# One decoder layer with routed experts on one core: query and key weights merged on chip, fewer VectorE steps, results stored by SyncE

## The chip, the core and the metric

The kernel runs on one core of a Trainium2 chip. A core has five engines, each with an instruction queue of its own that is worked off in order: TensorE (PE; its weight loads are shown apart as PEld), VectorE (DVE), ScalarE (ACT), GpSimd (POOL) and SyncE (SP), which here only issues DMAs. Engines wait for each other through semaphores. Matmuls write to PSUM, everything else lives in SBUF, and the inputs, the results and two large tables of rows lie in HBM. The metric is the device time of one execution in microseconds (us).

## What is computed

A decoder layer over 16 sequences of 256 tokens with 256 features, all in float32. It has three parts, each followed by a residual and a layer norm:

```python
# 1. linear attention, 16 heads of 16: q, k = elu(.) + 1
x = norm(x + linear_attention(x, w_qkv, w_out, b_out))
# 2. cross-attention to 77 context rows a sequence, one head of 256
q = x @ Wq.T + bq
k = ctx @ Wk.T + bk
v = ctx @ Wv.T + bv
x = norm(x + softmax(q @ k.T) @ v)
# 3. a block with routed experts
a = attention(norm(x) * ln1_w + ln1_b)   # 16 heads of 16, 4 groups
h = x + a @ proj.T
y = norm(h) * ln2_w + ln2_b
gate = softmax(y @ router.T)             # 8 experts, the best 2
moe = sum over the best 2 of gate[e] * (gelu(y @ w1[e]) @ w2[e])
x = norm(x + h + moe)
```

In the attention of part 3 the causal axis is the sequence index (16), not the token: token t of sequence s sees token t of sequences 0 to s. So sequences are worked off in order, and the work of this attention grows with s.

## The kernel before

Four generators ("strands") are interleaved, each a step further on for one sequence: `beginning` (linear attention, `linear_attention`), `crossing` (`context_keys` for every second sequence, then `cross_attention`), `scoring` (`scores`: the projections of part 3 and the products of queries with all keys so far) and `routed` (`values`, then the router, then `place`). A scheduler fixes the order of each engine's queue when the program is built; scores and values carry a lower priority, the experts' blocks one lower still, so that they fill what the rest leaves.

**Cross-attention.** For each pair of sequences `context_keys` projects the context of both (154 columns) with the key weights on PE (tile pk) and adds the bias on DVE (L396, tile kT). Per sequence `cross_attention` projects the context's values, transposes x on PE, projects queries (pq from `wq_sb`), adds their bias on ACT (L411, tile q), multiplies q by kT (psc), takes the maximum on DVE (L417) and the exponential on ACT (L421), transposes it and multiplies by the values. All its PSUM tiles come from the pool `ps_x`, which has one buffer.

**Part 3's attention** runs on DVE: products and sums over 16 positions (L453, L497, L526). The sum of the exponentials divides the result at L528, on 512 elements a partition.

**Routing.** `router` finds the two best experts (L562, L563) and writes a mask `hot` (L565, L568). `place` gives each token a row in the table `slots_in`: it counts the tokens ahead with two bfloat16 matmuls (L600, L601), one over the current tile (m), one over all tiles before (cm, carried from sequence to sequence by L594 and L598), adds the expert's first row (L603), picks the two rows of each token (L607, L609), casts them (L611) and scatters (L616, indirect DMAs on POOL). `dispatch` and `pick` choose blocks of 128 rows for which an expert can run, and `experts` runs these: xs loaded by SP, transposed, two matmul layers (L287 as ph, L871 as po), rows stored to `slots_out` by SP. SP reads each block's place from a register first. `behind(...)` keeps SP's loads and stores in an order written out by hand.

**The end.** The sequences form two turns, of 13 and of 3 sequences. After a turn's experts, `combined` works on pairs of sequences: it gathers each token's two rows (L903, indirect DMAs on POOL, 52 and 12 of them), adds them to the residual on DVE (L916), and normalizes with `normalized(..., late=True)`: mean and variance on DVE, `shift` = -mean on DVE (L302), rstd on POOL (L303 adds epsilon, L308 takes the power -0.5, L311 multiplies the shift), the result on DVE (L316). `store` writes the pair to `out`, on POOL's queue (L924); only the last store goes by SP. POOL's and SP's queues are thus both shared between transfers and other work.

**Tables cleared.** The tables are cleared in pieces during `beginning`: `clear_piece` makes a tile of zeros from the layer norm's output on DVE (L251), so that each clearing DMA on SP starts only when that sequence is through.

Of the kernel before, what the change touches and what calls it, by code (L numbers as in the profile page):

```python
# [15 lines left out]
P = 128  # L16
# [22 lines left out]
W1S = 2  # L39
YS = 3  # L40
# [26 lines left out]
def decoder_kernel(  # L67
# [46 lines left out]
    def chunked(src, width, name):  # L114
        t = const.tile([P, src.shape[0] // P, width], FP, name=name)
        ins = load(t, src.rearrange("(c p) o -> p c o", p=P))
        return t, ins
# [22 lines left out]
    wk_sb, _ = chunked(wkT, D, "wk_sb")  # L140
    wv_sb, _ = chunked(wvT, D, "wv_sb")
    wq_sb, _ = chunked(wqT, D, "wq_sb")
# [67 lines left out]
    nc.gpsimd.tensor_copy(ones_c, ones)  # L210
    n_picks = max(k for turn in TURNS for of in picks(turn) for k in of)
# [3 lines left out]
    nc.vector.tensor_copy(count, count_i)  # L215

# [30 lines left out]
    def clear_piece(x1):  # L247
        if not to_clear:
            return
        zeros = one.tile([P, D], FP, tag="zeros", name=f"zeros_{len(to_clear)}")  # L250
        nc.vector.tensor_scalar(zeros, x1[:, 0, :], 0.0, None, ALU.mult)  # L251
        for rows_of in to_clear.pop(0):
            rows_of = rows_of.rearrange("(p r) d -> p r d", p=P)
            nc.sync.dma_start(
                out=rows_of, in_=zeros.unsqueeze(1).to_broadcast([P, rows_of.shape[1], D])
            )


    at_all = const.tile([P, S * NT, 2], FP_I, name="at_all")
    ws_all = const.tile([P, S * NT, NE], FP, name="ws_all")  # L260

# [27 lines left out]
    def normalized(dst, src, name, late=False, again=None):  # L289
# [12 lines left out]
        nc.vector.tensor_scalar(shift[:, :nt], mv[:, :nt, 0], -1.0, None, ALU.mult)  # L302
        nc.gpsimd.tensor_scalar(rstd[:, :nt], mv[:, :nt, 1], EPS, None, ALU.add)  # L303
# [7 lines left out]
        nc.gpsimd.tensor_tensor(shift[:, :nt], shift[:, :nt], rstd[:, :nt], ALU.mult)  # L311
        for i in range(n - 1, -1, -1):
            to = dst[i] if i < nt else again[i - nt]
            r, s = rstd[:, i : i + 1], shift[:, i : i + 1]
            if late:
                nc.vector.tensor_scalar(to, src[i % nt], r, s, ALU.mult, ALU.add)  # L316
            else:
                nc.scalar.activation(to, src[i % nt], AF.Identity, bias=s, scale=r)  # L318
# [14 lines left out]
    def linear_attention(b, xb):  # L333
# [52 lines left out]
        normalized(tiles(y), tiles(y), f"n1_{b}")  # L386
        return y

    def context_keys(b0, ct):

        pk = ps_x.tile([P, NC, 2 * CTX], FP, tag="pm", name=f"pk_{b0}")
        kT = two.tile([P, NC, 2 * CTX], FP, tag="kT", name=f"kT_{b0}")
        for j in range(NC):
            project(pk[:, j, :], lambda c: wk_sb[:, c, bass.ts(j, P)], lambda c: ct[:, c, :])
        for j in range(NC):
            nc.vector.tensor_scalar(kT[:, j, :], pk[:, j, :], bk[:, j : j + 1], None, ALU.add)  # L396
        return kT

    def cross_attention(b, x1, ct, kT):
# [6 lines left out]
        pq = ps_x.tile([P, NC, N], FP, tag="pm", name=f"pq2_{b}")  # L406
        for j in range(NC):
            project(pq[:, j, :], lambda c: wq_sb[:, c, bass.ts(j, P)], lambda c: xT[:, c, :])
        q = one.tile([P, NC, N], FP, tag="q2", name=f"q2_{b}")
        for j in range(NC):  # L410
            nc.scalar.activation(q[:, j, :], pq[:, j, :], AF.Identity, bias=bq[:, j : j + 1])  # L411
        yield
        psc = ps_x.tile([P, NT, CTX], FP, tag="pm", name=f"psc_{b}")
        for t in range(NT):
            project(psc[:, t, :], lambda c: q[:, c, bass.ts(t, P)], lambda c: kT[:, c, own])
        nmax = small.tile([P, NT], FP, tag="nmax", name=f"nmax_{b}")
        nc.vector.tensor_reduce(nmax, psc, AX.X, ALU.max, negate=True)  # L417
        p = one.tile([P, NT, CTX], FP, tag="p2", name=f"p2_{b}")
        total = small.tile([P, NT], FP, tag="total", name=f"total_{b}")
        for t in range(NT):  # L420
            nc.scalar.activation(  # L421
                p[:, t, :],
                psc[:, t, :],
# [77 lines left out]
    def values(s, x2, sc):  # L501
# [11 lines left out]
        nc.vector.reciprocal(total, total)  # L513
        yield
# [3 lines left out]
        with tc.high_priority(offset=-BULK):  # L518
# [8 lines left out]
        attn3 = attn.rearrange("p t (h d) -> p (t h) d", d=HD)  # L527
        nc.vector.tensor_tensor(  # L528
            attn3, attn3, total.unsqueeze(2).to_broadcast([P, NT * H, HD]), ALU.mult
        )  # L530
# [9 lines left out]
    def router(xT, top, hot, name):  # L540
# [23 lines left out]
        idx_f = small.tile([P, NT, 2], FP, tag="idx_f", name=f"idx_f_{name}")  # L564
        nc.vector.tensor_copy(idx_f, idx[:, :, :2])  # L565
        for t in range(NT):
            shape = [P, 2, NE]
            nc.vector.tensor_tensor(  # L568
                hot[:, t, :, :],
                count[:, :NE].unsqueeze(1).to_broadcast(shape),  # L570
                idx_f[:, t, :].unsqueeze(2).to_broadcast(shape),
                ALU.is_equal,
            )
# [12 lines left out]
    def place(u, d, b, t0, y4, hot, state):  # L586

        grid = [P, NT, NE]
        m = small.tile(grid, COUNT, tag="dm", name=f"dm_{b}")
        nc.vector.tensor_tensor(m, hot[:, :, 0, :], hot[:, :, 1, :], ALU.add)  # L590

        cm = two.tile([P, NT + 1, NE], COUNT, tag="dcm", name=f"dcm_{b}")
        if t0:
            nc.vector.tensor_copy(cm[:, 0, :], state["cm"])  # L594
        else:
            nc.vector.memset(cm[:, 0, :], 0.0)
        for t in range(NT):
            nc.vector.tensor_tensor(cm[:, t + 1, :], cm[:, t, :], m[:, t, :], ALU.add)  # L598
        pc = ps_b.tile([P, NT + 1, NE], FP, tag="pm", name=f"pc_{b}")
        nc.tensor.matmul(pc, lhsT=ones_c, rhs=cm, start=True, stop=False)  # L600
        nc.tensor.matmul(pc[:, :NT, :], lhsT=earlier_c, rhs=m, start=False, stop=True)  # L601
        slot = small.tile(grid, FP, tag="slot", name=f"slot_{b}")
        nc.vector.tensor_tensor(  # L603
            slot, pc[:, :NT, :], first_slot[u].unsqueeze(1).to_broadcast(grid), ALU.add
        )
        of = small.tile([P, NT, 2, NE], FP, tag="of", name=f"of_{b}")
# [426 lines left out]
```

## Time and profile before

| | |
|---|---|
| median of 3 runs | 821.78 us (819.98 to 822.94) |
| the profiled execution | 823.85 us, its span 822.0 us |
| busy: PE, PEld | 693.7 us, 552.2 us |
| busy: DVE, ACT, POOL | 601.9 us, 453.8 us, 303.1 us |
| mean granted clock of PE | 0.948 |
| HBM | 112.33 MB, 137 GB/s over the span |

The span runs from the first to the last instruction. A row of a group names the line, the engine and the operation, what it writes and reads, and how often; behind the bar stand the busy time and the mean of one (in ns), then the idle time just before. A float32 matmul stands as two records, a transpose as one. A line of a helper gathers all that the helper records (L287 is `project`), so groups are told apart by tiles. Durations of short instructions on one engine overlap: what a small step costs there is nearer to the distance of two starts.

### The profile page before, as it was taken

What the parts mean: (1) busy time and instruction counts of PE and PEld (TensorE: products, weight loads), DVE (VectorE), ACT (ScalarE), POOL (GpSimd) and SP (SyncE); (2) the same over time, 40 slices, a digit from 0 to 9 for tenths busy, and PEclk for the clock granted to TensorE, in tenths of its full rate; (3) what the DMA queues carried; (4) which work ended last, traced back from release to release, by engine and by line L of the source; (5) the groups of instructions that cost most, each with busy time, mean ns of one, the idle gap of its engine ahead of it and who ended that gap; (6) DMA issues with size and microseconds to landing.
All of it is one profiled execution on the core that took longest, in us unless ns stands there. A gap on an engine that the chain in (4) does not pass through costs nothing. (4 is left out here: it accounts for less than half of the span.)

```text
span 822.0 us, 12778 instructions
## 1 busy us (share of the span) xinstructions
PE 693.7 (84%) x3676; PEld 552.2 (67%) x3676; DVE 601.9 (73%) x1571; ACT 453.8 (55%) x967; POOL 303.1 (37%) x400
## 2 busy tenths in 40 slices
PE   6888878798899798989998989989789998989700
PEld 4656656566676676867786877768677887789600
DVE  2345758868898998979899978989899940334444
ACT  2354535545656667564956566485865665545300
POOL 2023224334343423334323332231333211588765
PEclk9999989989999999999999989999999999999955
DMA  8946454364353251721353412413333221555533
GB/s 279 392 166 217 139 188 151 102 204 156 104 198 115 85 193 41 241 72 66 119 164 110 134 52 90 129 58 122 91 103 88 95 70 66 167 178 152 161 107 101
DMA packets 98115, 112.33 MB, mean 137 GB/s; under 512 B 6336, under 2 KB 90560, under 8 KB 98048
## 3 DMA queue, kind: packets, MB, share of 16 engines
q1 hardware_dynamic: 90704, 90.81, 33.6%
q0 software_dynamic: 7344, 20.72, 7.9%
q8 instruction: 31, 0.51, 0.3%
q14 instruction: 36, 0.29, 0.1%
HBM read 39.42 MB, written 72.09 MB: 136 GB/s over the span
## 5 line engine op out<-in xcount | busy, mean ns | idle before, releaser
L287 PE MATMUL ph<-xsT,w 128*128 128x128 f32 (+1 forms) x976 | 160.9, 309 | 6.8 <-ACT xsT L831 3.5
L871 PE MATMUL po<-we_sb,h 128*128 x624 | 158.7, 386 | 6.2 <-ACT ys L879 2.3
L287 PEld LDWEIGHTS ph<-xsT,w 128*128 128x128 f32 x976 | 135.3, 193 | 21.9 <-ACT xsT L831 9.4
L616 POOL DMA_INDIRECT slots_in<-y,at_all x64 | 77.4, 1210 | 167.2 <-ACT h L862 35.8
L871 PEld LDWEIGHTS po<-we_sb,h 128*128 128x128 f32 x624 | 111.5, 193 | 22.5 <-issue 2.7
L453 DVE TENSOR_TENSOR qk<-q,k_all 128x128 f32<-128x128 f32 (+15 forms) x64 | 82.3, 1285 | 18.9 <-ACT k_all L481 18.2
L862 ACT ACTIVATE h<-ph 128x512 f32<-128x512 f32 x78 | 46.5, 597 | 85.1 <-PE ph L287 78.8
L453 DVE TENSOR_TENSOR pv<-sc,v_all 128x128 f32<-128x128 f32 (+15 forms) x64 | 82.9, 1295 | 0.4
L497 DVE TENSOR_REDUCE sc<-qk 128x8 f32<-128x128 f32 (+15 forms) x64 | 81.8, 1278 | 0.8
L526 DVE TENSOR_REDUCE attn<-pv 128x128 f32<-128x128 f32 (+15 forms) x64 | 81.6, 1275 | 0.5
L743 POOL TENSOR_TENSOR x<-x,y 128x512 f32<-128x512 f32 x16 | 27.6, 1728 | 134.9 <-DVE y L537 134.9
L815 ACT COPY w<-we_sb 128x1024 f32 x61 | 63.9, 1047 | 10.7 <-PE ph L287 9.6
L287 PE MATMUL pkv<-wqkv_sb,tT_x 128*128 128x512 f32 x128 | 61.4, 602 | 0.0
L287 PE MATMUL pq<-wqkv_sb,tT_n 128*128 128x384 f32 x128 | 54.1, 547 | 8.2 <-ACT tT_n L467 4.6
L384 POOL TENSOR_TENSOR x<-xb,rows_sb 128x512 f32<-128x512 f32 x16 | 24.5, 1533 | 81.1 <-DVE x L441 47.7
L308 POOL TENSOR_TENSOR rstd_n<-rstd_n,neg_half 128x2 f32<-128x2 f32 (+1 forms) x57 | 51.2, 898 | 4.4
L831 ACT ACTIVATE xsT<-px,cols_sb 128x256 f32<-128x256 f32 (+1 forms) x80 | 41.0, 564 | 13.0 <-PE px L828 13.0
L903 POOL DMA_INDIRECT r<-slots_out,at_all x36 | 35.4, 983 | 32.2 <-issue 32.2
L303 POOL TENSOR_SCALAR rstd_n<-mv_n 128x2 f32<-128x2 f32 (+1 forms) x57 | 19.6, 344 | 72.4 <-DVE mv_n L299 68.7
L318 ACT ACTIVATE x<-x,shift_n,rstd_n 128x256 f32<-128x256 f32 x64 | 35.0, 593 | 10.4 <-POOL shift_n L311 10.2
L316 DVE TENSOR_SCALAR res<-res,rstd_n,shift_n 128x256 f32<-128x256 f32 x32 | 11.7, 424 | 38.5 <-POOL shift_n L311 38.5
L287 PEld LDWEIGHTS pq<-wqkv_sb,tT_n 128*128 128x128 f32 x128 | 24.9, 209 | 22.0 <-ACT tT_n L467 6.3
(257 smaller groups left out, 1389.8 us busy)
## 6 DMA issues: line engine op xcount, KB each, us to landing
slots_out<-zeros SPq DMA_DIRECT2D x10, 3328.0 KB, 12.0
we_sb<-in_w SPq DMA_DIRECT2D x16, 512.0 KB, 9.0
slots_in<-zeros SPq DMA_DIRECT2D x2, 3328.0 KB, 12.3
xs<-slots_in SPq DMA_DIRECT2D x44, 128.0 KB, 2.1
slots_out<-ys SPq DMA_DIRECT2D x44, 128.0 KB, 1.8
xs<-slots_in SPq DMA_DIRECT2D x17, 256.0 KB, 2.8
slots_out<-ys SPq DMA_DIRECT2D x17, 256.0 KB, 2.2
xb<-in_x SPq DMA_DIRECT2D x16, 256.0 KB, 2.8
```

The source lines that it names most:

```text
L287: nc.tensor.matmul(dst, lhsT=lhsT(c), rhs=rhs(c), start=(c == 0), stop=(c == NC - 1))
L308: nc.gpsimd.tensor_tensor(rstd[:, :n], rstd[:, :n], neg_half[:, :n], ALU.pow)
L318: nc.scalar.activation(to, src[i % nt], AF.Identity, bias=s, scale=r)
L453: nc.vector.tensor_tensor(pr, a.to_broadcast(shape), b.to_broadcast(shape), ALU.mult)
L497: nc.vector.tensor_reduce(scr[:, :, r, :], pr, AX.X, ALU.add)
L526: nc.vector.tensor_reduce(attnr[:, :, r, :], pr, AX.X, ALU.add)
L616: scatter = nc.gpsimd.indirect_dma_start(out=scatters[u][2 * (t0 + t) + i], out_offset=bass.IndirectOffsetOnAxis(ap=at[:, t, i : i + 1], a ...
L815: nc.scalar.copy(w.rearrange("p c f -> p (c f)"), we_sb[:, bass.ds(off, NC * FF)])
L831: nc.scalar.activation(xT[:, c, : nt * P], px[:, c, : nt * P], AF.Identity, bias=ln2_b[:, c : c + 1], scale=ln2_w[:, c : c + 1],)
L862: nc.scalar.activation(h[:, fs.start : fs.stop, at], ph, AF.Gelu_apprx_tanh)
L871: nc.tensor.matmul(po[:, t, :], lhsT=h[:, f, bass.ts(t, P)], rhs=we_sb[:, bass.ds(off + (NC * FF + f * D), D)], start=(f == 0), stop=(f == ...
L903: nc.gpsimd.indirect_dma_start(out=r[:, t, i, :], out_offset=None, in_=slots_out[u], in_offset=bass.IndirectOffsetOnAxis(ap=at_all[:, b * ...
```

## The change

The kernel is changed in these places.

- **One matrix for queries and keys.** q k^T = (x Wq^T + bq)(c Wk^T + bk)^T = x (Wq^T Wk) c^T + x Wq^T bk + (bq Wk) c^T + bq bk. `merged_weights` makes Wq^T Wk and the bias parts on chip, once, before the first keys: eight transposes, fourteen small matmuls, copies on DVE. kT then has a third row of tiles, the part that depends only on the context row, repeated over all partitions. The query projection and its bias go; x transposed is multiplied by kT itself, and DVE adds the third row before the maximum (p). kT's bias is added on ACT. `wk_sb` and `wq_sb` are loaded into buffers that other tiles use later.
- **Fewer DVE steps.** `hot` in one compare without a cast; the counts ahead are carried in the row number itself (`state["next"]`, a row more in `slot`), so that cm goes and a third count matmul comes; the rows are summed straight into integers; the softmax of part 3 is divided before the values instead of after; zeros are made once; late norms use (x - mean) * rstd, with epsilon added on DVE and only the power left to POOL.
- **Results by SP.** `store` goes to SP's queue. In turn 0 it holds eight sequences back (LATE pairs) and puts the rest behind the loads; the remaining ones follow the last expert store.

```diff
+LATE = 4
...
-    wk_sb, _ = chunked(wkT, D, "wk_sb")
+    wk_sb, _ = chunked(wkT, D, "wk_sb", one, "q2")
+    wq_sb, _ = chunked(wqT, D, "wq_sb", one, "attnb")
     wv_sb, _ = chunked(wvT, D, "wv_sb")
-    wq_sb, _ = chunked(wqT, D, "wq_sb")
...
+    zeros = const.tile([P, D], FP, name="zeros")
+    nc.gpsimd.memset(zeros, 0.0)
+
+    def clear_piece(after):
...
-        zeros = one.tile([P, D], FP, tag="zeros", name=f"zeros_{len(to_clear)}")
-        nc.vector.tensor_scalar(zeros, x1[:, 0, :], 0.0, None, ALU.mult)
...
+            tc.add_manual_dep(ins.ins, after.ins.name, landed, reason="bandwidth")
...
-        nc.vector.tensor_scalar(shift[:, :nt], mv[:, :nt, 0], -1.0, None, ALU.mult)
-        nc.gpsimd.tensor_scalar(rstd[:, :nt], mv[:, :nt, 1], EPS, None, ALU.add)
+        if late:
+            nc.vector.tensor_scalar(rstd[:, :nt], mv[:, :nt, 1], EPS, None, ALU.add)
+        else:
+            nc.vector.tensor_scalar(shift[:, :nt], mv[:, :nt, 0], -1.0, None, ALU.mult)
+            nc.gpsimd.tensor_scalar(rstd[:, :nt], mv[:, :nt, 1], EPS, None, ALU.add)
...
-        nc.gpsimd.tensor_tensor(shift[:, :nt], shift[:, :nt], rstd[:, :nt], ALU.mult)
+        if not late:
+            nc.gpsimd.tensor_tensor(shift[:, :nt], shift[:, :nt], rstd[:, :nt], ALU.mult)
...
-                nc.vector.tensor_scalar(to, src[i % nt], r, s, ALU.mult, ALU.add)
+                nc.vector.tensor_scalar(to, src[i], mv[:, i, 0:1], r, ALU.subtract, ALU.mult)
...
+    def merged_weights():
+        wT = []
+        for w, name in ((wk_sb, "wk"), (wq_sb, "wq")):
+            t = two.tile([P, NC, D], FP, tag="sc", name=f"{name}T")
+            nc.vector.tensor_copy(t, transposed(ps_a, w, name))
+            wT.append(t)
+        wkT_, wqT_ = wT
+        for c in range(NC):
+            pm = ps_a.tile([P, D + 1], FP, tag="pm", name=f"pm_{c}")
+            own = bass.ts(c, P)
+            project(pm[:, :D], lambda d: wkT_[:, d, own], lambda d: wqT_[:, d, :])
+            project(pm[:, D:], lambda d: wkT_[:, d, own], lambda d: bq[:, d : d + 1])
+            nc.vector.tensor_copy(m_sb[:, c, :], pm[:, :D])
+            nc.vector.tensor_copy(mq_sb[:, c, :], pm[:, D:].to_broadcast([P, P]))
+        pb = ps_a.tile([P, NC + 1], FP, tag="pm", name="pm_b")
+        for c in range(NC):
+            own = bass.ts(c, P)
+            project(pb[:, c : c + 1], lambda d: wqT_[:, d, own], lambda d: bk[:, d : d + 1])
+        project(
+            pb[:, NC:],
+            lambda d: bq[:, d : d + 1].to_broadcast([P, P]),
+            lambda d: bk[:, d : d + 1],
+        )
+        nc.vector.tensor_copy(mb_sb, pb)
...
-            project(pk[:, j, :], lambda c: wk_sb[:, c, bass.ts(j, P)], lambda c: ct[:, c, :])
-        for j in range(NC):
-            nc.vector.tensor_scalar(kT[:, j, :], pk[:, j, :], bk[:, j : j + 1], None, ALU.add)
+            project(pk[:, j, :], lambda c: m_sb[:, c, bass.ts(j, P)], lambda c: ct[:, c, :])
+        project(pk[:, NC, :], lambda c: mq_sb[:, c, :], lambda c: ct[:, c, :])
+        for j in range(NC + 1):
+            nc.scalar.activation(kT[:, j, :], pk[:, j, :], AF.Identity, bias=mb_sb[:, j : j + 1])
...
-        pq = ps_x.tile([P, NC, N], FP, tag="pm", name=f"pq2_{b}")
-        for j in range(NC):
-            project(pq[:, j, :], lambda c: wq_sb[:, c, bass.ts(j, P)], lambda c: xT[:, c, :])
-        q = one.tile([P, NC, N], FP, tag="q2", name=f"q2_{b}")
-        for j in range(NC):
-            nc.scalar.activation(q[:, j, :], pq[:, j, :], AF.Identity, bias=bq[:, j : j + 1])
...
-            project(psc[:, t, :], lambda c: q[:, c, bass.ts(t, P)], lambda c: kT[:, c, own])
+            project(psc[:, t, :], lambda c: xT[:, c, bass.ts(t, P)], lambda c: kT[:, c, own])
+        nc.vector.tensor_tensor(p, psc, kT[:, NC, own].unsqueeze(1).to_broadcast(shape), ALU.add)
...
+        nc.vector.tensor_tensor(
+            sc3, sc3, total.unsqueeze(2).to_broadcast([P, NT * H, n]), ALU.mult
+        )
...
-        nc.vector.tensor_tensor(
-            attn3, attn3, total.unsqueeze(2).to_broadcast([P, NT * H, HD]), ALU.mult
-        )
...
-        cm = two.tile([P, NT + 1, NE], COUNT, tag="dcm", name=f"dcm_{b}")
...
-        nc.tensor.matmul(pc, lhsT=ones_c, rhs=cm, start=True, stop=False)
+        nc.tensor.matmul(pc, lhsT=ones_c, rhs=behind_none, start=True, stop=False)
+        nc.tensor.matmul(pc[:, NT, :], lhsT=ones_c, rhs=m[:, 0, :], start=False, stop=False)
         nc.tensor.matmul(pc[:, :NT, :], lhsT=earlier_c, rhs=m, start=False, stop=True)
...
+        first = state["next"] if t0 else first_slot[u]
+        nc.vector.tensor_tensor(slot, pc, first.unsqueeze(1).to_broadcast(shape), ALU.add)
+        state["next"] = slot[:, NT, :]
...
-        nc.vector.tensor_copy(at, at_f)
-        total = small.tile([P, NE], FP, tag="cnt_f", name=f"cnt_f_{b}")
-        nc.vector.tensor_copy(total, pc[:, NT, :])
...
-        def store(pair, queue=nc.gpsimd):
-            for b in pair:
-                queue.dma_start(out=out[b].rearrange("(t p) d -> p t d", p=P), in_=acc[b])
+            owed.extend((b, acc[b]) for b in pair)
+
+        def store(most, after):
+            while len(owed) > most:
+                b, of = owed.pop(0)
+                with behind(after[-1:]):
+                    nc.sync.dma_start(out=out[b].rearrange("(t p) d -> p t d", p=P), in_=of)
...
-                if i == 0 and n > 1:
-                    store(pairs[n - 2])
             if n:
                 add(pairs[n - 1])
+            if b1 < S:
+                store(2 * LATE, loads)
+            elif n == 0:
+                store(0, stores)
             yield
-        if len(pairs) > 1:
-            store(pairs[-2])
         add(pairs[-1])
-        store(pairs[-1], nc.sync if b1 == S else nc.gpsimd)
+        if b1 == S:
+            store(0, stores)
```

## The prediction

> **What bounds the kernel now.** I read the busy rows of the page first: which engine is full, and when.
>
> ```profile
> PE   6888878798899798989998989989789998989700
> ...
> DVE  2345758868898998979899978989899940334444
> ...
> PEclk9999989989999999999999989999999999999955
> ```
>
> Each digit is a fortieth of the span (20.5 us). PE and DVE are both near nine tenths from slice 10 to 31, counted from 0; neither alone is the bound. After slice 37 PE does nothing, while the span goes on for 46 us. Busy time by stage gives the sizes (columns: time, PE, PEld, DVE, ACT, POOL, granted clock, DMA):
>
> ```profile
> 200.00:640.00 440.00, 404.96 (x2097) 321.99 (x2097) 400.84 (x911) 284.46 (x601) 146.59 (x172) 0.98 0.36 115
> ...
> 704.00:776.00 72.00, 69.34 (x459) 62.44 (x457) 31.52 (x100) 36.90 (x58) 58.15 (x67) 0.98 0.54 162
> 776.00:823.00 47.00, 0.00 (x0) 0.00 (x0) 21.72 (x70) 0.85 (x2) 29.15 (x40) 0.54 0.36 115
> ```
>
> In the middle stage PE is 92% busy and DVE 91%: work taken from one alone would leave the other in the way. Work taken from both should come through. From 704 us on the chain of waits names POOL almost throughout: 64 gathers of expert rows, in order on one queue. The POOL timeline of the end shows what stands between them (start, length):
>
> ```profile
> 781.48 1.03 POOL L903 DMA_INDIRECT r<-slots_out,at_all  x1 [0.18 <-issue]
> 782.53 1.06 POOL L308 TENSOR_TENSOR rstd_n<-rstd_n,neg_half 128x4 f32<-128x4 f32 x1
> ...
> 793.97 0.72 POOL L308 TENSOR_TENSOR rstd_n<-rstd_n,neg_half 128x2 f32<-128x2 f32 x1
> 794.77 0.19 POOL L311 TENSOR_TENSOR shift_n<-shift_n,rstd_n 128x2 f32<-128x2 f32 x1
> 796.03 0.77 POOL L924 DMA_DIRECT2D out<-res  x1 [1.07 <-DVE res L316]
> 797.11 1.07 POOL L903 DMA_INDIRECT r<-slots_out,at_all  x1 [0.31 <-issue]
> ```
>
> The 52 gathers of turn 0 begin at 703.73 and end at 782.5; the 12 of turn 1 wait until 797.11 behind three normalizations and five stores of results. The last of the 61 expert stores (L885) starts at 783.3; with its 0.36 us and the 1.9 us to landing that these stores take in the middle, rows are there at 785.6, so 11.5 us of the end are queue order alone.
>
> **The change part by part.** The groups by shape give durations (busy us, mean ns):
>
> ```profile
> L287 PE MATMUL pq<-tT_x,wq_sb 128*128 128x256 f32 x128 | 34.4, 409 | 0.1
> ...
> L528 DVE TENSOR_TENSOR attn<-attn,total 128x512 f32<-128x512 f32 x16 | 11.0, 688 | 0.2
> ...
> L396 DVE TENSOR_SCALAR kT<-pk,cols_sb 128x154 f32<-128x154 f32 x16 | 5.6, 356 | 0.0
> ...
> L598 DVE TENSOR_TENSOR dcm<-dcm,dm 128x8 bf16<-128x8 bf16 x32 | 5.1, 159 | 0.6
> ```
>
> *PE in the body.* The query projection goes: 8 records a sequence. In the PE timeline such a run starts at 31.72 and the next work at 33.55, so 1.83 us, times 16 is 29.3. Added per pair of sequences is a third context projection, half of the 1.21 us that the 8 records of pk take at 70.19, times 8 is 4.8. Added per sequence is a count matmul of 8 columns: its nearest rows, pc at 640.01 and 640.04, start 0.03 apart but show 0.18 plus a weight load of 0.10, so between 0.03 and 0.28; I take 0.1, as they run back to back, times 16 is 1.6. Net: 29.3 - 4.8 - 1.6 = 22.9 us less PE.
>
> *DVE in the body.* Small steps cost their spacing, not their duration: `slot` 229.56 minus 0.10, `of` 229.67, about 0.10 apart while each row says 0.16 to 0.19. Per sequence go two dcm adds, one dcm copy, the casts idx_f and at_f, the copy cnt_f, and one of two hot compares: 7 x 0.10 x 16 = 11.2 (17 by durations). kT moves to ACT: 5.6. The zeros (L251) go: 4.3. The division by the softmax sum works on 32n elements instead of 512: the nearest row, the subtraction on the same tile, has a median of 0.46 against 0.688, so 16 x 0.23 = 3.7. Added is p = psc + bias over 154 elements, between L417 (0.311) and L396 (0.356) on the same shape: 16 x 0.33 = 5.3. The rstd step that the late normalization moves to DVE replaces the shift step there. Net: 11.2 + 5.6 + 4.3 + 3.7 - 5.3 = 19.5 us less DVE.
>
> *ACT.* L411 goes (13.6 us); 24 kT evictions come, at 0.39 each (between 128x77 with 0.325 and 128x256 with 0.476): 9.3. ACT is 65% busy in the middle, so I cost the move at nothing; PE and DVE hide it. If that cover were gone, a kT that is 3 x 0.39 instead of 2 x 0.33 late costs 0.5 us a pair, 4 us in all.
>
> *What comes through.* The lesser saving is 19.5; with each engine full for about 0.9 of the body, and the static queues between them, I take 16. Bounds: 0, if the freed time all becomes waiting, and 26, if the shorter chain (no query projection, no 0.84 us bias step on ACT at 33.76 between transposes and scores) also takes waits away.
>
> *The start.* The PE queue of the changed kernel puts the merging of the weights between po of sequence 0 and the transposes of sequence 1, and nothing else can pass: sequence 0 waits for kT, sequence 1 stands behind it.
>
> ```profile
> 22.14 3.59 PE L287 MATMUL po<-wout_sb,tT_a 128*128 128x256 f32 x8 [0.68 <-ACT tT_a L282]
> 25.53 0.73 PE L276 MATMUL pt_x<-ident,xb 128*128 128x128 f32 x4
> 26.99 1.99 PE L287 MATMUL pq<-tT_x,wqkv_sb 128*128 128x256 f32 x8 [0.73 <-DVE st_n L298]
> ```
>
> Eight transposes: 2 x 0.73 = 1.5. Four matmuls of 256 columns, 8 records: 2.0. Ten of one column, 20 records, by the nearest row (pl, 8 columns, 8 records in 1.06): 2.65. The first kT, now here: 1.2 + 0.6. Exposed on DVE: one 128x512 copy 0.69, one 128x256 eviction 0.42, and four hand-overs of some 0.2: 1.9. Together 9.9. The old kT's wait for its weights (1.78) and its 0.69 no longer stand before the keys of sequence 0: 9.9 - 2.5 = 7.4; I take 8. Bounds: 3, since PE had 4.7 us idle from 30 to 60 that can absorb part, and 14, since the first row above shows 3.59 for the work that takes 1.99 elsewhere, so PE's part of 8 can cost nearly twice as much.
>
> *The end.* POOL loses 15 stores (0.78 each), the rstd and the shift steps, and keeps pow. 52 gathers at their spacing of 1.25 are 65.0, with four pows of 1.1 between them 69.4 instead of 78.8. From there the old chain takes 14.6 to 797.11; without shift, store and its wait of 1.07, the gather follows the last pow (794.7 instead of 797.1), and two earlier rounds lose 0.2: 12. So the last gathers could start 81.4 us after the first instead of 93.4. The last expert store lands 81.9 after it, and becomes the later one: 11.5 saved, less 0.5 that the new SP work may cost it. I take 11.
>
> *SP's queue.* It takes 15 more stores. Two pairs stand before the store of ys_1_0 and before the second of ys_1_1; behind them wait these, the loads xs_1_7 and xs_1_8, and through three ys buffers ACT and PE. Pair 0 is normalized about 18 x 1.25 + 2.5 = 25 us after the first gather, pair 1 about 40 after. In the PE timeline px of block pairs 7 and 8 run 51 and 58 after it, ys_1_4 is wanted at about 51: cover of 10 us and more, so I cost it at nothing; gone, each us goes to the last store. The other stores stand behind all expert stores. Bounds for the end: 12 saved, or 0.
>
> Sum against the profiled execution's own 823.85 (span 822.0 and 1.85 around it): 823.85 - 16 + 8 - 11 = 804.85. The median of the runs is 2.07 lower, 821.78; in its terms 802.8, forecast as 803.
>
> **A rule that speaks against it.** PE's granted clock falls after idle stretches (columns as before):
>
> ```profile
> 285.00:290.00 5.00, 2.47 (x9) 1.17 (x8) 4.60 (x22) 4.41 (x13) 1.13 (x3) 0.86 0.10 35
> 290.00:295.00 5.00, 5.00 (x19) 3.57 (x18) 4.52 (x11) 3.90 (x10) 1.53 (x2) 0.80 1.04 348
> ```
>
> PE was idle 2.5 us, and 0.14 x 5 + 0.20 x 5 = 1.7 us of clock went. About ten such places are in the trace. The Trainium skill, "TensorE: Matmul & The Clock Gate", "Why this matters for your kernels", says to leave no gaps of over about 3 us between bursts, since one idle window puts the clock back to half. By that rule, if every sequence's hole passed the length, the sum would be 802.8 + 27 = 830; by the row, 802.8, until a gap opens.
>
> **Rivals.**
> - *Only the end counts.* The body is bound by waits between strands, its freed work turns idle (4 of 16 come). For it: PE's idle time has a dozen causes, the largest pt_n waiting for ACT with 10.1 us in the middle. Against: the two full rows. 823.85 - 4 + 8 - 11 = 816.9, or 814.8 against the median.
> - *Slower: clock.* Nothing of the body comes through, and the hole of the query projection becomes a dip in each of 16 sequences: 16 x 1.7 = 27. 823.85 + 27 + 8 - 11 = 847.9, or 845.8. It decides from 11 more dips on, where the forecast's 19 is eaten. Against: experts' matmuls fill PE from 250 us on.
> - *The end doesn't do what it says.* The normalizations come later than the cover, SP holds back expert stores, and the end saves nothing: 815.9, or 813.8.
>
> **How the numbers follow.** Forecast 0.66, only the end 0.13, end unchanged 0.10, slower 0.11. A difference within 0.3% (2.5 us) can't be told here. The forecast's own range is its bounds less their extremes, 788 to 813. To leave out no more than two in ten, the range goes from 786 (body 26, start 3, end 12 gives 786.8) to 821. Of the milder cases 0.05 may end within 0.3%: faster 0.84, same 0.05, slower 0.11.
>
> **What would show it.** PE's busy time falls by some 17 (22.9 less the 1.5 + 2.0 + 2.65 of merging), DVE's by some 17 to 20 (19.5 less the merging's copies). The transposes of sequence 1 start near 33.5. The first gather of turn 0 comes near 696 instead of 703.73, the first of turn 1 some 82 after it. SP's stores wait for DVE without PE starving between px 6 and 8. Wrong would be: more low clocks in the middle, or PE idle grown by as much as its work fell.

## The result, and the profile after

The changed kernel takes 816.24 us (median of 20 runs, 811.84 to 824.34), the kernel before 824.32 us beside it (20 runs, 818.99 to 829.07). The ratio is 0.9912, 95% interval 0.9891 to 0.9932: 0.9% less, or some 7 us (the medians lie 8 us apart). One of the changed kernel's runs, 824.34 us, was a slow one and is left out of the ratio. Forecast were 19 us. The profiled execution took 818.29 us with a span of 816.4, against 823.85 and 822.0 before: 5.6 us less.

The page of the changed kernel, busy times (time, share, records):

```profile
PE 691.5 (85%) x3632; PEld 546.3 (67%) x3632; DVE 589.3 (72%) x1451; ACT 449.7 (55%) x961; POOL 287.0 (35%) x369
...
PE   6888898788889899989998989989788998796940
...
DVE  1245875877896888989898988989978972153555
...
PEclk9899997998996999989999999999989999998985
```

PE's busy time fell from 693.7 to 691.5 us, not by the 17 that the prediction counts. The records did go (3676 to 3632). The ones that are left run longer: the row PEclk has seven digits under 9 up to slice 36 where the row before has three. The same stages as before, in windows (time, PE, PEld, DVE, ACT, POOL, granted clock, DMA):

```profile
200.00:640.00 440.00, 397.95 (x2053) 314.54 (x2052) 384.98 (x801) 275.94 (x587) 142.98 (x169) 0.96 0.34 109
704.00:776.00 72.00, 63.11 (x421) 56.77 (x420) 32.34 (x104) 36.58 (x56) 53.48 (x55) 0.95 0.53 155
...
776.00:823.00 47.00, 8.58 (x47) 7.11 (x45) 20.49 (x65) 2.75 (x5) 17.36 (x19) 0.68 0.39 125
```

In the middle PE lost 7 us of busy time and DVE 16, at a clock of 0.96 instead of 0.98. And PE now works past 776 us, where it was done before.

Four marks split the span; the body is taken from the transposes of sequence 1 to the first gather, the end from there to the last instruction:

| mark (us) | before | after | difference |
|---|---|---|---|
| transposes of sequence 1 | 25.53 | 34.16 | +8.6 (forecast +8) |
| body | 678.2 | 669.6 | -8.6 (forecast -16) |
| first gather of turn 0 | 703.73 | 703.73 | 0 |
| end | 118.3 | 112.7 | -5.6 (forecast -11) |

The busy times of the body, first before, then after (columns as above):

```profile
25.53:703.73 678.20, 607.66 (x3158) 478.19 (x3157) 543.68 (x1384) 410.01 (x897) 209.65 (x270) 0.97 0.39 129
34.16:703.73 669.57, 594.54 (x3073) 464.14 (x3071) 528.01 (x1255) 403.25 (x887) 208.49 (x268) 0.95 0.39 126
```

The start is as foreseen, the body and the end give half. The PE timeline of the start, changed kernel (start, length):

```profile
25.36 1.06 PE L288 MATMUL pt_wk<-ident,wk_sb 128*128 128x128 f32 x4
...
28.52 1.13 PE L299 MATMUL pm<-wqT,wkT 128*128 128x256 f32 x4 [1.07 <-DVE wqT L413]
...
34.16 0.60 PE L288 MATMUL pt_x<-ident,xb 128*128 128x128 f32 x4
```

Four transposes cost 1.06 us where the last line shows 0.60 for four: the clock is at half here. The POOL timeline of the end, changed kernel:

```profile
776.60 0.96 POOL L940 DMA_INDIRECT r<-slots_out,at_all  x1 [0.31 <-issue]
777.58 1.04 POOL L323 TENSOR_TENSOR rstd_n<-rstd_n,neg_half 128x4 f32<-128x4 f32 x1
784.61 1.11 POOL L323 TENSOR_TENSOR rstd_n<-rstd_n,neg_half 128x4 f32<-128x4 f32 x1 [5.98 <-DVE rstd_n L315]
788.75 0.69 POOL L323 TENSOR_TENSOR rstd_n<-rstd_n,neg_half 128x2 f32<-128x2 f32 x1 [3.04 <-DVE rstd_n L315]
791.52 1.01 POOL L940 DMA_INDIRECT r<-slots_out,at_all  x1 [2.08 <-DMA out<-res]
```

The stores are gone from POOL's queue, and in their place POOL waits for DVE: 5.98 and 3.04 us. So its last three powers are as far apart as before (7.0 and 4.1 us against 6.9 and 4.5). The first gather of turn 1 comes 87.8 us after the first of turn 0 (forecast 82, before 93.4).

### The profile page after: what moved, and what is told of

The parts are those of the page before. It is cut to its first block, busy times and chain, and to the rows that moved or that the text cites. A ratio compares the mean times of both kernels' runs of the same rounds, so it can differ in the third digit from the quotient of the medians.

```text
span 816.4 us, 12518 instructions
## 1 busy us (share of the span) xinstructions
PE 691.5 (85%) x3632; PEld 546.3 (67%) x3632; DVE 589.3 (72%) x1451; ACT 449.7 (55%) x961; POOL 287.0 (35%) x369
## 5 line engine op out<-in xcount | busy, mean ns | idle before, releaser
L299 PE MATMUL ph<-xsT,w 128*128 128x128 f32 (+1 forms) x976 | 163.9, 315 | 14.1 <-ACT ys L916 6.2
L908 PE MATMUL po<-we_sb,h 128*128 x624 | 156.3, 387 | 7.1 <-ACT xsT L868 3.0
L299 PEld LDWEIGHTS ph<-xsT,w 128*128 128x128 f32 x976 | 138.4, 199 | 29.7 <-ACT xsT L868 8.9
L498 DVE TENSOR_TENSOR pv<-sc,v_all 128x128 f32<-128x128 f32 (+15 forms) x64 | 84.6, 1322 | 0.6
L299 PE MATMUL pq<-wqkv_sb,tT_n 128*128 128x384 f32 x128 | 58.2, 584 | 9.4 <-ACT tT_n L512 8.3
L323 POOL TENSOR_TENSOR rstd_n<-rstd_n,neg_half 128x2 f32<-128x2 f32 (+1 forms) x57 | 50.2, 881 | 17.2 <-DVE rstd_n L315 13.1
L940 POOL DMA_INDIRECT r<-slots_out,at_all x36 | 35.2, 976 | 33.0 <-issue 27.2
L294 ACT COPY tT_a<-pt_a 128x512 f32<-128x512 f32 x32 | 18.7, 584 | 46.8 <-PE pt_a L288 46.7
L288 PE MATMUL pt_n<-ident,y 128*128 128x128 f32 x128 | 21.2, 289 | 27.3 <-ACT y L334 27.3
L299 PEld LDWEIGHTS pq<-wqkv_sb,tT_n 128*128 128x128 f32 x128 | 26.7, 223 | 24.6 <-ACT tT_n L512 10.3
```

What stands on the lines that cost most here:

```text
L299: nc.tensor.matmul(dst, lhsT=lhsT(c), rhs=rhs(c), start=(c == 0), stop=(c == NC - 1))
L323: nc.gpsimd.tensor_tensor(rstd[:, :n], rstd[:, :n], neg_half[:, :n], ALU.pow)
L498: nc.vector.tensor_tensor(pr, a.to_broadcast(shape), b.to_broadcast(shape), ALU.mult)
L908: nc.tensor.matmul(po[:, t, :], lhsT=h[:, f, bass.ts(t, P)], rhs=we_sb[:, bass.ds(off + (NC * FF + f * D), D)], start=(f == 0), stop=(f == ...
L940: nc.gpsimd.indirect_dma_start(out=r[:, t, i, :], out_offset=None, in_=slots_out[u], in_offset=bass.IndirectOffsetOnAxis(ap=at_all[:, b * ...
```

## The experiments

Ratios are to the kernel before, with 95% intervals. Clock is the median over the runs of the mean granted clock. Body and end (first gather of turn 0 to first of turn 1) come from one profile each, in us.

| kernel | ratio | clock | body | end |
|---|---|---|---|---|
| before | 1 | 0.949, 0.947 | 678.2 | 93.4 |
| the change | 0.9912 (0.9891 to 0.9932) | 0.941 | 669.6 | 87.8 |
| merged matrix alone | 1.0096 (1.0068 to 1.0125) | 0.934 | 679.3 | 93.9 |
| change without it | 0.9876 (0.9845 to 0.9907) | 0.960 | 682.3 | 86.0 |
| the end alone | 0.9932 (0.9903 to 0.9961) | 0.951 | 678.5 | 86.5 |
| query projection back, unread | 1.0360 (1.0330 to 1.0391) | 0.933 | 707.7 | 87.0 |
| LATE = 7 | 0.9901 (0.9866 to 0.9936) | 0.940 | 665.7 | 86.4 |
| merging in PE's gaps | 0.9831 (0.9791 to 0.9870) | 0.948 | 668.2 | 87.2 |
| matmuls in the gaps | 1.0044 (1.0020 to 1.0068) | 0.953 | 675.4 | 88.4 |
| no merging, LATE = 7, order | 0.9902 (0.9864 to 0.9939) | 0.957 | 675.6 | 86.3 |

**The parts, one by one.** Merged matrix alone, on the kernel before:

> The kernel before with the merged weight matrix alone; the DVE steps, the late norm, the zeros and the stores stay as before. By the prediction's terms: PE 24.5 us less in the body (29.3 - 4.8), DVE about the same (kT 5.6 goes, p 5.3 comes), start +8. Theory A (PE and DVE are both full, only what both lose comes through): the body gains about nothing, so 5 to 9 us slower than before. Theory B (PE's work counts by itself): 10 to 16 us faster than before. Theory C (PE's freed time becomes gaps in which its granted clock falls): as A or worse, with a mean granted clock at least 0.01 under the kernel before.

It is 1% slower, theories A and C. The start is 7.2 us late (32.76), and 24.5 us less of PE (by the prediction's terms) bring nothing in the body: DVE is busy there for 545.2 us against 543.7, and the clock is 0.015 lower. The change without the merged matrix:

```diff
-            project(pk[:, j, :], lambda c: m_sb[:, c, bass.ts(j, P)], lambda c: ct[:, c, :])
+            project(pk[:, j, :], lambda c: wk_sb[:, c, bass.ts(j, P)], lambda c: ct[:, c, :])
...
+            project(pq[:, j, :], lambda c: wq_sb[:, c, bass.ts(j, P)], lambda c: xT[:, c, :])
```

> The change without the merged matrix: queries and keys are projected as before, all other parts (DVE steps, zeros, late norm, stores by SP) stay. Theory A (the merging costs its 8 us at the start and gives little in the body): 4 to 8 us faster than the change, so 808 to 812 where the change has 816. Theory B (the merging pays in the body more than its start): 3 to 12 us slower than the change. In the trace the transposes of sequence 1 should be back near 25.5 us.

0.9876 against 0.9912: some 3 us faster than the change, with overlapping intervals, and the transposes of sequence 1 at 23.59. That is theory A's way, a little under its 4 to 8 us. The 682.3 in the table is from a run of 818.53 us, where the median is 813.04. The end alone, on the kernel before:

> The kernel before with the end's part alone: late norms by (x - mean) * rstd with epsilon on DVE, and results stored by SP. Prediction: 11 us faster than before, the first gather of turn 1 about 82 us after the first of turn 0. Theory S (SP's stores of results stand before stores of expert rows and hold PE back): 3 to 7 us faster, gather about 87 after, and PE idle for some 5 us waiting for ACT's copy of expert rows. Theory T (PE's tail was late in the change only because its body was): 10 to 12 us faster, no such wait.

5.6 us faster (0.0068 of 822), a distance of 86.5 and a wait of PE of 4.4 us on ACT's copy of expert rows: theory S by its numbers, and as much as the end of the change has saved. Beside it, the change without the merging tells what the DVE steps are worth by the runs: 0.9932 to 0.9876, some 4.6 us.

**What PE's work is worth.** The query projection put back behind the transposes, unread:

```diff
         xT = transposed_sb(ps_x, x1, f"x1_{b}")
+        pq = ps_x.tile([P, NC, N], FP, tag="pm", name=f"pq2_{b}")
+        for j in range(NC):
+            project(pq[:, j, :], lambda c: m_sb[:, c, bass.ts(j, P)], lambda c: xT[:, c, :])
```

> The change with the 128 matmul records of the query projection put back at their old place, on the merged matrix, with nobody reading them: 29.3 us of PE at full clock are added, no other work. Theory A (PE's work counts in full, as the prediction's 22.9 assumed on its side): 20 to 29 us slower than the change. Theory W (PE's freed time is idle time between waits): 0 to 5 us slower. Theory C (the freed time also lets the granted clock fall): within 3 us of the change or faster, with the mean granted clock up by 0.01 or more.

Theory A and more: 0.0448 of 822 is 37 us for 29.3 us of matmuls, and the clock falls instead of rising. PE's work at this place costs its full time and more. But PE's load isn't all that changes: the tile pq takes the only buffer of `ps_x` between the transposes and the scores, so each sequence's chain grows too, and the two aren't told apart. Nor does load alone set the body. With busy time at half clock counted half, PE has 591.7 us of work in this body against 589.8 before, and DVE is busy 10.8 us less; yet the body is 29.5 us longer than before, since half clock costs PE 15.4 us more and PE is idle 12.2 us more. What in the changed order makes these waits isn't shown. Then two matmuls ahead of each group of transposes that waits for a norm (`warm` is that norm's tile of means and variances, so they start when it is there):

```diff
+        for i in range(2 if warm is not None else 0):
+            nc.tensor.matmul(
+                pt[:2, 0, :], lhsT=warm[:, 1, :], rhs=wout_sb[:, 0, :], start=True, stop=True
+            )
```

> The change with two matmuls of 256 columns added ahead of the transposes that wait for ACT's normalized rows (two places a sequence, 64 matmuls, some 29 us of PE at full clock), on a PSUM tile that the transposes overwrite; they start when the mean and variance are there, so they lie in the gap in which PE waits. Theory C (the gaps ahead of these transposes let the granted clock fall, and the fall eats the gain): the clock rises by 0.01 or more, the time is at most 3 us over the change's, perhaps under it. Theory A (PE's work counts, wherever it stands): 15 to 29 us slower, clock no higher.

The same 29 us cost 11 here (1.0044 against 0.9912), and the clock rises by 0.012. Neither theory holds alone. In the body of the profile PE's work, counted as above, grows by 32.7 us against the change; half clock costs PE 17.4 us less, and its idle time falls by 9.5: most of the filler lies in gaps or is paid by the higher clock, the rest counts. The waits that it fills, PE from 60 to 704 us (us in total, times, longest), first before, then the change:

```profile
PE pt_n L276 <- ACT y L318: 17.3, 19, 2.4
```

```profile
PE pt_n L288 <- ACT y L334: 26.3, 26, 2.4
```

**The start.** The merging's PSUM tiles from the experts' pool instead of the linear attention's:

```diff
-            pm = ps_a.tile([P, D + 1], FP, tag="pm", name=f"pm_{c}")
+            pm = ps_e.tile([P, D + 1], FP, tag="pe", name=f"pm_{c}")
```

> The change with the merging's PSUM tiles taken from the pool of the experts' blocks, which is empty at the start, instead of from the pool of the linear attention: nothing ties the merging to the end of sequence 0's linear attention any more, and the scheduler puts it into PE's gaps between 10 and 22 us. Theory A (the start costs some 8 us because the merging stands alone on PE, at a low clock): the transposes of sequence 1 come near 28 to 30 us instead of 34.2, and the time is 3 to 6 us under the change's. Theory B (the start is made up for later, by waits): same within 1.5 us.

Theory A, and a little over its 3 to 6 us: 0.9831, 6.7 us under the change, the fastest kernel here. The PE timeline of this kernel:

```profile
15.80 0.60 PE L288 MATMUL pt_wq<-ident,wq_sb 128*128 128x128 f32 x4
...
18.28 1.03 PE L299 MATMUL pm<-wqT,wkT 128*128 128x256 f32 x4
19.14 1.09 PE L384 MATMUL pn<-kv,q 128*128 128x136 f32 x8
...
27.32 0.60 PE L288 MATMUL pt_x<-ident,xb 128*128 128x128 f32 x4
```

The merging stands between steps of sequence 0 at the full clock (0.60 for four transposes), and sequence 1 starts 6.8 us earlier than in the change. About as much arrives at the end of the kernel; the intervals leave some 4 us open, and the clock is 0.007 higher too.

**The end.** All results of turn 0 behind the last expert store:

> The change with LATE = 7 instead of 4: all results of turn 0 stand on SP behind the last store of expert rows. Theory S (SP's result stores, waiting for DVE's normalization, hold the expert rows' stores, through three buffers ACT and PE, and PE's tail): PE's wait for ACT's copy of 5.46 us at 743.5 and the low clock behind it go, PE ends near 776 instead of 785, and the last expert store is issued some 7 us earlier; the time is 2 to 6 us under the change's (816.2). Theory T (the hold costs nothing, the end is set by POOL's and DVE's normalizations): same within 1.5 us.

Theory T by its time: 0.9901 against 0.9912 is no difference. Yet what theory S says of PE did happen. In the PE timeline of the change:

```profile
742.08 1.46 PE L908 MATMUL po<-we_sb,h 128*128 x6
749.01 0.80 PE L299 MATMUL ph<-xsT,w 128*128 128x128 f32 x2 [5.46 <-ACT ys L916]
```

and in SP's queue, where the stores of pair 1 stand ahead of three stores of expert rows:

```profile
743.96 0.92 SPq L965 DMA_DIRECT2D out<-res  x2
745.12 6.14 SPq L922 DMA_DIRECT2D slots_out<-ys  x3
```

With LATE = 7 the wait is gone and PE ends 71.9 us after the first gather of turn 0 instead of 81.2. But POOL reaches turn 1's first gather at 86.4 instead of 87.8: the hold was nearly hidden. What is left of it stands in SP's queue, the last store of expert rows:

```profile
788.98 0.33 SPq L922 DMA_DIRECT2D slots_out<-ys  x1
```

Its landing is recorded at 790.7, after POOL's last power (over at 789.4), and the gather at 791.52 needs these rows. The view puts the 2.08 us down to a store of results; by the semaphores POOL stood for this landing until 790.7. With LATE = 7 the last such store is issued at 775.65, and the gather starts 0.30 us after the power.

What POOL waits for earlier shows in the change, first on DVE, then on POOL:

```profile
763.94 0.17 DVE L315 TENSOR_SCALAR rstd_n<-mv_n 128x4 f32<-128x4 f32 x1
764.01 0.48 DVE L953 SCALAR_TENSOR_TENSOR res<-r,ws_all,res 128x256 f32<-128x256 f32 x1
768.92 1.38 DVE L332 TENSOR_SCALAR res<-res,mv_n,rstd_n 128x256 f32<-128x256 f32 x4 [4.43 <-POOL rstd_n L323]
770.22 2.06 DVE L953 SCALAR_TENSOR_TENSOR res<-r,ws_all,res 128x256 f32<-128x256 f32 x5
```

```profile
766.87 0.95 POOL L940 DMA_INDIRECT k_all<-slots_out,at_all  x1 [0.30 <-issue]
767.84 1.05 POOL L323 TENSOR_TENSOR rstd_n<-rstd_n,neg_half 128x4 f32<-128x4 f32 x1
772.56 1.01 POOL L940 DMA_INDIRECT r<-slots_out,at_all  x1 [3.68 <-DVE res L953]
```

The variance is ready at 764.1. POOL's power stands behind gathers until 767.84, DVE stands at the norm's last step until 768.92, the next pair's additions stand behind it, and POOL's next gather waits until these free the buffer r. Without merging, with LATE = 7, and with turn 1's gathers ahead of the last norm in program order:

> The change without the merged matrix, with LATE = 7, and with the first gathers of turn 1 put ahead of the last normalization of turn 0 on POOL and DVE. The change without the merging alone had 813.0 beside 822.45 of the kernel before. If the hold on SP (2 to 6 us) and the order on POOL (up to 5 us) each count: 803 to 809. If the end is set by DVE's last normalizations: 811 to 814.

0.9902 (815.2 us, above both ranges), no gain over the same body with LATE = 4 (0.9876). The scheduler put the gathers behind the powers all the same (787.65, after a power at 786.78), so the order stays untested.

**Runs that the end spoiled.** In the ten runs that follow, the kernel before took 841.5 to 848.9 us beside them, and kernels with the new end took 130 to 139 us between the first gather and the first of turn 1. Of these runs only the body and the ratio to the kernel before beside them are read.

| kernel | ratio to the kernel before beside it | body | end |
|---|---|---|---|
| LATE = 7, last step deferred | 1.0219 (1.0177 to 1.0262), 1.0291 (1.0265 to 1.0316) | 672.0, 669.7 | 137.6, 139.4 |
| merging in gaps, LATE = 7, deferred | 1.0146 (1.0093 to 1.0199), 1.0178 (1.0148 to 1.0209), 1.0199 (1.0148 to 1.0249) | 671.1, 667.2, 666.2 | 137.9, 137.5, 136.8 |
| the same without merging | 1.0254 (1.0212 to 1.0295) | 672.3 | 137.6 |
| without the context's own part | 1.0125 (1.0081 to 1.0168), 1.0152 (1.0115 to 1.0190) | 657.5, 662.7 | 130.3, 136.3 |
| merging in gaps, that part by PE | 1.0174 (1.0137 to 1.0210) | 670.6 | 136.9 |
| merging in gaps, end as before | 0.9898 (0.9861 to 0.9935) | 670.1 | 119.3 |

The deferred step, meant for the chain of POOL and DVE above (`settle` does the last step of the pair before):

```diff
+            finish = normalized(all_t, all_t, f"n5_{pair[0]}", late=True)
+            settle()
+            unfinished.append((finish, [(b, acc[b]) for b in pair]))
```

> The change with LATE = 7 and with each pair's last step of the late norm, (x - mean) * rstd on DVE, put behind the additions of the next pair instead of ahead of them. Theory K (POOL and DVE hold each other in the end: DVE stands at the last step of a pair until POOL's power is done, POOL's power stands behind gathers of the next pair, the next pair's additions stand behind DVE, and POOL's gather of the pair after that waits for their buffer): POOL's waits of 3.7, 6.0 and 3.0 us shrink by 4 us or more in all, the first gather of turn 1 comes 80 to 83 us after the first of turn 0 instead of 86.4, and the time is 3 to 6 us under that of LATE = 7 alone (0.9901 of the kernel before). Theory D (the waits are DVE's own work and the landing of the gathers): 85 to 87 us, same time within 1.5 us.

> Early merging, LATE = 7 and the deferred step together, a third time. On a chip where the kernel before takes 822 to 824 us: theory K (POOL and DVE hold each other in the end) gives 80 to 83 us from the first gather of turn 0 to the first of turn 1 and a ratio of 0.975 to 0.980; theory D (DVE's own work and the landings) gives 85 to 87 us and 0.982 to 0.984. On a chip like the last two: again some 137 us and a ratio of 1.015 to 1.018.

Neither theory can be read at 137 us; whether deferring helps stays open. Without the part of the scores that depends on the context row alone:

> The change without the part of the scores that depends on the context row alone: no third projection of the context (32 records of PE), no third part of kT on ACT, no addition of it on DVE; the maximum and the exponential read PSUM as before. This part of the scores is left out. By the prediction's terms 4.8 us of PE and 5.3 us of DVE. Theory P (the step on DVE between the scores and their maximum, and what it does to the order, costs what the merging should have gained): 6 us or more under the change's time, clock up. Theory Q (it is worth its durations at most): 1 to 5 us under the change's.

The ratio can't be read, the body can: 657.5 and 662.7, on average 8.8 us under the change's body (nine profiles of it, here and above, have a mean of 668.9). That is over theory Q's 1 to 5 us and within theory P's 6 or more; but P's higher clock isn't seen (43.1 and 65.2 us at half clock in these two bodies, 41.0 to 61.4 in the nine). The prediction priced this part at 4.8 us of PE and 5.3 of DVE, 10.1 together; here, where work goes from both engines, nearly the sum is gained, not the lesser of the two. Whether the load does it or the shorter chain (8 evictions less on ACT, a step less before the maximum) these runs don't tell. The early merging, LATE = 7 and the deferred step without the merging, for what the merging is worth:

> As the early merging with LATE = 7 and the deferred step, but without the merged matrix. It tells what the merging is worth where its start is hidden. The change without the merging had 0.9876 of the kernel before, the early merging 0.9831. Theory M (the merging saves 4 to 6 us in the body once its start is hidden): 3 to 7 us slower than its counterpart with the merging. Theory N (the merging is worth nothing): within 2 us of it.

It has 1.0254 where its counterpart beside it has 1.0146, some 9 us slower: theory M's way, above its 3 to 7 us. The context's own part added by PE instead of DVE:

> The early merging with the context's own part of the scores added by PE (one more accumulating matmul of ones with kT's third row, 64 records of 77 columns, some 6.8 us of PE) instead of by DVE (5.3 us); the maximum and the exponential read PSUM as in the kernel before. Theory P (the DVE step in the chain is the harm): 2 to 8 us under the early merging alone (0.983 of the kernel before), so 0.974 to 0.981. Theory A (PE's work counts in full, DVE's a quarter): 3 to 7 us over it, 0.987 to 0.992.

The body is 670.6, within the spread of the other nine (665.7 to 672.0): moving 5 us from DVE to PE changes nothing that one profile can show, and theory P's 2 to 8 us aren't seen. The body without merging has 682.3, 675.6 and 672.3, a mean of 676.7; beside the other steps the merging is worth 7.8 us of body, with three profiles that lie 10 us apart. Last, the early merging with results and late norms as before:

> The early merging and the DVE steps of the change with the end of the kernel before (results stored from POOL's queue, late norm with shift and rstd on POOL). On a chip where the kernel before takes 822 to 824 us: the end's 5.6 us are missing, ratio 0.988 to 0.992 (early merging alone 0.983). On a chip where it takes 840 us or more: theory G (the loss there comes with the new end, which leaves POOL nothing but gathers) gives a ratio of 0.985 to 0.995 there too, and from the first gather of turn 0 to the first of turn 1 some 115 us or less; theory H (it comes with any kernel of this body) gives 1.01 to 1.02 and some 137 us.

Theory G by its ratio: 0.9898, where the kernel before took 848.9 us. The distance of the first gathers is 119.3 us, over its 115 and far under theory H's 137.

## Why the prediction was wrong

The direction and the start were right, and that the body and the end gain; both terms were mis-sized, because the sum put the clock, a wait for DVE and the hold on SP at nothing.

**The body, "I take 16": 8.6.** The step that failed is the clock: "by the row, 802.8, until a gap opens" puts it at nothing. Count PE's busy time in the body with the time at half clock taken half, from the records of both traces. This work falls from 589.8 to 567.3 us, by 22.5, as forecast (22.9). What half clock costs PE rises from 17.9 to 27.2 us, and its idle time from 70.5 to 75.1: 22.5 - 9.3 - 4.6 = 8.6. The forecast had 6.9 us for waiting and none for the clock. This adds up what happened; it doesn't show that without the dips all 9.3 us would be gained. A second estimate: the kernel before is at half clock for 37.8 us within the body, the change for 61.4, merged matrix alone for 61.4. Over the nine profiles of the change's body, a line through them rises by 0.25 us of body for each us at half clock; so 23.6 us more are some 6 of the 7.4 us that are missing.

DVE's term was mis-sized too: its busy time in the body falls by 15.7 us (543.68 to 528.01), not 19.5. That work taken from both engines counts most was right: the merging alone gains nothing in the body (679.3 against 678.2), the DVE steps alone leave it at a mean of 676.7, together it is 668.9, that is 9.3 less. The query projection put back shows that the load isn't all.

One dip of the clock in the change, PE timeline and windows (columns as above):

```profile
125.03 0.66 PE L288 MATMUL pt_n<-ident,y 128*128 128x128 f32 x4 [2.44 <-ACT y L334]
```

```profile
120.00:125.00 5.00, 2.60 (x16) 2.13 (x14) 4.94 (x12) 2.09 (x5) 3.23 (x6) 1.00 0.02 3
125.00:130.00 5.00, 4.17 (x23) 3.75 (x24) 2.06 (x14) 3.60 (x11) 1.12 (x3) 0.62 0.00 0
130.00:135.00 5.00, 4.72 (x13) 2.87 (x14) 0.67 (x5) 2.84 (x9) 2.70 (x3) 0.50 0.89 280
```

PE idles for 2.44 us, and then works for 10 us at half speed though it is 83% to 94% busy. This is also how 44 records could go with 2.2 us of busy time. The length of the gap alone doesn't decide: in the kernel before PE idles for 2.99 us from 587 on, and the clock from 587 to 597 is 1.00. Over the 20 runs of the change the span falls by 6.5 us for each 0.01 of mean clock (correlation -0.88), over 17 of the kernel before by 4.9. The rule of the Trainium skill that was weighed ("TensorE: Matmul & The Clock Gate", "Why this matters for your kernels": no gaps of over about 3 us) named the right danger. The price by the row was one dip of 1.7 us; here a dip of 10 us followed a gap of 2.44, shorter than the rule's length. Its sum of 830 was as wrong as the 803 that left the dips out. The rival "slower: clock" had the mechanism, not the size. The rival "only the end counts" has the nearest time (814.8), by luck: the body gave 8.6 us, not 4, and the end 5.6, not 11.

**The end, "I take 11": 5.6**, the same in the end alone. The step "52 gathers at their spacing of 1.25 are 65.0, with four pows of 1.1 between them 69.4" held no wait for DVE. The last gather of turn 0 is over 73.8 us after the first; of the 4.4 us more, 3.7 are the wait for the buffer r. Before, stores and shift steps stood between the gathers and no gather waited for a buffer; taken away, they uncovered the next limit. From there to turn 1 it takes 14.0 us instead of 12.0. The powers come as the prediction has them; the rest is the landing of the last store of expert rows. With LATE = 7, where this store is early, it takes 12.2.

**SP's queue, cost at nothing: some 1.4 us** between the profiles of the change and of LATE = 7. The cover was mis-stated: ys was wanted 40 us after the first gather, not 51, and pair 1's result was ready just then. PE stood 5.46 us, and the last store of expert rows became late by it. It cost little only because POOL was late too.

**The start, 8: 8.6.** Other profiles with this start have sequence 1 at 31.6 to 34.2, that is 6.1 to 8.6 us later than before. It is paid: with the early merging 6.8 us earlier went with 6.7 us less time.

**PE's and DVE's busy times.** DVE's fell by 12.6 us instead of 17 to 20: 15.7 less in the body, 3.5 more ahead of it. PE's fell by 2.2 instead of 17: its work at full clock by 15.3 (672.5 to 657.2), and half clock took 13.1 of that back.

## What to carry to other kernels

Work taken from one of two full engines may buy nothing by itself, as the merging alone did; sum what leaves both, and look what the clock does with the holes: compare PE's busy time with its count of records. One-time work at the start cost about its full length here, until other buffers let it slip into gaps that were already there; changing the pool of its PSUM tiles was worth nearly as much as the whole change. And where stores are moved off a queue, ask which wait they had been hiding, and what stands behind them on the queue that takes them.

## What the hardware showed

The time of one kernel can change from one time of measuring to the next: the kernel before took 821.8 to 824.3 us at some and 841.5 to 848.9 at others (medians). Where it took the longer time, PE and ACT did nothing for tens of us while the gathers ran. Windows of the early merging with LATE = 7 and the deferred step, then of the one with the old end:

```profile
715.00:725.00 10.00, 0.00 (x0) 0.00 (x0) 6.23 (x20) 0.00 (x0) 7.95 (x9) 0.50 0.33 93
725.00:735.00 10.00, 0.00 (x0) 0.00 (x0) 4.07 (x14) 0.00 (x0) 8.15 (x8) 0.50 0.32 92
```

```profile
715.00:725.00 10.00, 0.00 (x0) 0.00 (x0) 2.47 (x6) 0.70 (x3) 8.33 (x10) 0.50 0.33 92
725.00:735.00 10.00, 7.69 (x34) 6.89 (x34) 4.82 (x18) 1.48 (x3) 8.26 (x10) 0.67 0.52 159
```

POOL goes on gathering in both, DMA is a third busy, and PE stands until 744 in the first and until 725 in the second; ACT's timeline in the first says 40.15 us of "issue", a wait for nothing that the profile shows. With the old end, whose POOL queue has stores and small steps between the gathers, the loss was about that of the kernel before (119.3 us between the first gathers instead of 93.4; 848.9 us instead of some 823). The cause isn't known, neither the change itself nor a kernel that won above was run under these conditions, and why other runs are free of it is open.
